# The tail of a fused attention and perception kernel: another order of its jobs, a fifth PSUM bank, results in tiles of their own

## The chip, the cores and the metric

The kernel runs on one core of one Trainium2 chip. The time is the device time of that core in microseconds, as a median of a few runs. The profile shows one more execution of the same kernel; its span runs from the first to the last instruction.

The engines are named as in the profile: PE (TensorE, matrix products), PEld (its weight loads), DVE (VectorE), ACT (ScalarE, which evaluates functions), POOL (GpSimd) and SP (SyncE, which issues the transfers here). PSUM has eight banks of 128 partitions by 512 float32 values; every product lands in one of them, and another engine has to read it out before the bank is used again.

## The reference

The input x has shape (4, 64, 64, 256): four images, 4096 pixels each, 256 channels. Everything is float32.

```python
# layer 0: attention of every pixel to every pixel of its image
q, k, v = x @ Wq + bq, x @ Wk + bk, x @ Wv + bv
attn = softmax(q @ k^T)
x = gamma * (attn @ v) + x
# layer 1: depthwise 3x3 convolution, two pointwise layers, local attention
perceived = conv3x3(x, w_perc, groups=256) + b_perc        # 768 channels
hid = gelu(w_up1 @ perceived + b_up1)                      # 512 channels
h = x + w_up2 @ hid + b_up2                                # 256 channels
q, k, v = split(w_qkv @ h + b_qkv)
w = softmax over the 3x3 neighbours of (q . k_neighbour) / 16
out = h + sum over the neighbours of w * v_neighbour
```

Neighbours outside the image have key and value zero, but they count in the softmax. So the result of a row needs the rows above and below it, both in the convolution and in the local attention.

## The kernel before

Channels lie on partitions. An image is cut into 8 blocks of 8 rows, 512 pixels each; over the four images this gives 32 blocks, which the code calls slots, 0 to 31. The function `unshifted` does everything, without subtracting a maximum in the softmax. It keeps a running sum `watched` of all intermediate values; at the end a flag `bad` says whether they stayed within bounds, and only if not a second, safe version runs. It does not run with these inputs, but the end of the program has to wait for the flag.

The **main loop** (lines 582 to 638) goes over the 32 slots. In each it runs the global attention of the slot's block on PE, and in between it weaves in layer 1 of blocks that are further back: the convolution of the block two slots back (`perceive`), the pointwise layers of the block three back (`hidden_jobs`), and the local attention of the block five back (`attention_jobs`). So at the end of the main loop these are left: the convolutions of blocks 30 and 31, the pointwise layers of 29, 30 and 31, and the local attention of 27 to 31. This is the **tail**, lines 641 to 656.

Instructions go to the engines in the order in which the Python code issues them (`tc.manual_schedule`); semaphores for tiles are put in by the framework. So the order of the jobs in the tail is the order of each engine's queue. The jobs are these; block numbers stand in brackets from here on.

- **hid** (`hidden`, four per block, line 310): six products of 512 columns into one bank on PE (two passes each, so twelve records), then a Gelu on ACT (line 319). They need all six results of the block's convolution.
- **upd** (`update`, two per block, line 321): four products of 512 columns into a bank, then one DVE instruction (line 331) that adds bias and x and writes one half of `h`.
- **new** (`local_values`, two per block, line 433): eight products of 256 columns that read both halves of `h`, and two DVE additions (line 446) to `lv` tiles.
- **guide** (two per block, line 395): two products of `h`, and an ACT instruction (line 405) that writes `lq`.
- **scores** (two, line 458): products of `h` and `lq`; an Exp on ACT (line 482); a multiplication with a mask on POOL (line 485). They read `h` of the next block too.
- **border and local_sum** (one job): four to eight small products, an Exp on ACT (line 429), and on POOL a multiplication (line 430), the sum of the two score tiles (line 494), small additions at the edge (lines 499 to 507) and an addition to `watched` (line 136).
- **local_denominator** (line 511, "ld" in the profile): one product with that sum, a reciprocal on DVE (line 515), and POOL's addition of it to `watched`.
- **local_product** (two, line 518, "lo"): twelve small products into a bank; DVE multiplies by the reciprocal (line 529) into a tile `o` of the two-buffer tag `lo`; POOL adds `o` to `watched` (`watch`, line 134); then `h` is added to `o` in place, on POOL for most blocks and on DVE for blocks 30 and 31 (line 532); and SP issues the transfer to the output (line 533).

`perceive` is a generator: for each of six results ACT does the first of nine taps (line 303), and DVE the other eight (line 307), one per call of `next`; so a block has 48 DVE steps. Since ACT's instruction is issued with the first step of its group, it stands in ACT's queue behind what was issued before.

In the tail each period k (29, 30, 31) runs the attention of block k-2 and the pointwise layers of block k alternately, with four steps of the convolution of block k+1 after each job. After the three periods come the attentions of blocks 30 and 31, and then the test of `watched` (lines 658 to 667). `job_bank` hands out the banks in turn; in the tail it takes "m" and "acc" (two banks each) alternately. The other four banks have the tag "e", for the energies of the global attention, which is over by then.

Of the kernel before, what the change touches and what calls it, by code (L numbers as in the profile page):

```python
# [8 lines left out]
F32 = mybir.dt.float32  # L9
AF = mybir.ActivationFunctionType  # L10
ALU = mybir.AluOpType
AX = mybir.AxisListType
PSUM = bass.MemoryType.PSUM

P = 128
# [5 lines left out]
NB = 512  # L21
# [4 lines left out]
TAPS = 9  # L26
MULT = 3
NPC = MULT * CH
# [3 lines left out]
GRP = P // CQK  # L32
NG = NT // GRP
NSLOT = B * NBLK

WATCH_MAX = 1.0e25

LAG_PERC, LAG_HID, LAG_ATT = 2, 3, 5
# [3 lines left out]
def attention_then_perception_kernel(  # L42
# [19 lines left out]
    nc = tc.nc  # L62
# [8 lines left out]
    ones = const.tile([P, P], F32, tag="ones", name="ones")  # L71
    watched = const.tile([P, NB], F32, tag="watched", name="watched")
    bad = const.tile([P, 1], mybir.dt.int32, tag="bad", name="bad")
# [3 lines left out]
    def unshifted():  # L77
        fctx = ExitStack()
        pool = fctx.enter_context(tc.tile_pool(name="fast", bufs=1))
        psum = fctx.enter_context(tc.tile_pool(name="fastp", bufs=1, space=PSUM))  # L80

        def tile_of(shape, tag, name, bufs=1):
            return pool.tile(shape, F32, tag=tag, name=name, bufs=bufs)

        def bank(tag, name):
            return psum.tile([P, NB], F32, tag=tag, name=name, bufs=2)
# [3 lines left out]
        turns = ["m"]  # L90

        def job_bank(name):
            turns.append(turns.pop(0))
            return bank(turns[-1], name)


# [21 lines left out]
        for half in range(2):  # L118
            m = near[half * W : (half + 1) * W]
            nc.gpsimd.affine_select(  # L120
                out=m, in_=m, compare_op=ALU.is_ge, fill=0.0,
# [3 lines left out]
                out=m, in_=m, compare_op=ALU.is_ge, fill=0.0,  # L125
# [8 lines left out]
        def watch(values):  # L134

            nc.gpsimd.tensor_tensor(watched, watched, values, ALU.add)  # L136
# [138 lines left out]
        percs, hids, hs = {}, {}, {}  # L275
        NPERC = NPC + 3

        def spare(name):
            return tile_of([P, TPB, C], "v", name, NBLK + 1).rearrange(
                "p (a t) c -> p a (t c)", a=2  # L280
            )

        def perceive(s):

            g = s % NBLK
            percs[s] = []
            for i in range(NPC):
                half, j = divmod(i, MULT)
                if s < NSLOT - LAG_PERC:
                    perc = tile_of([P, NB], "perc", f"perc_{s}_{i}", NPERC)  # L290
                else:

                    if i % 2 == 0:
                        pair = spare(f"perc_{s}_{i}")
                    perc = pair[:, i % 2, :]
                percs[s].append(perc)
                acc = perc.rearrange("p (h w) -> p h w", w=W)
                for tap in range(TAPS):
                    dy, dx = divmod(tap, 3)
                    win = xv[:, half, g * RB + dy : g * RB + dy + RB, dx : dx + W]  # L300
                    wt = wperc[:, half, j, tap : tap + 1]
                    if tap == 0:
                        nc.scalar.activation(  # L303
                            acc, win, AF.Identity, bias=bperc[:, half, j : j + 1], scale=wt
                        )
                    else:
                        nc.vector.scalar_tensor_tensor(acc, win, wt, acc, ALU.mult, ALU.add)  # L307
                        yield
# [86 lines left out]
        def guide(s, i):  # L395

            ps = job_bank(f"g_{s}_{i}")
            for kin in range(CH):
                nc.tensor.matmul(  # L399
                    ps, lhsT=wg[:, kin, bass.ts(i, P)], rhs=hs[s][:, kin, :],  # L400
                    start=(kin == 0), stop=(kin == CH - 1),
                )
            if i == 0:
                guides[s] = tile_of([P, CH, NB], "lq", f"lq_{s}")
            nc.scalar.activation(guides[s][:, i, :], ps, AF.Identity, bias=bg[:, i : i + 1])
# [42 lines left out]
        def pieces(s, odd):  # L448

            g = s % NBLK
            for t in range(-1 if odd else 0, TPB + 1, 2):
                lo, hi = max(0, (2 * t - 1) * W), min(NB, (2 * t + 3) * W)
                inside = 0 <= TPB * g + t < NT
                yield TPB * s + t if inside else None, slice(lo, hi)
# [54 lines left out]
        def local_denominator(s):  # L511
            ps = job_bank(f"ld_{s}")
            nc.tensor.matmul(ps, lhsT=ones, rhs=lsums.pop(s), start=True, stop=True)  # L513
            lrdens[s] = tile_of([P, NB], "rden", f"lrden_{s}", 2)
            nc.vector.reciprocal(lrdens[s], ps)  # L515
            watch(lrdens[s])

        def local_product(s, c):
            b, g = divmod(s, NBLK)
            ps = job_bank(f"lo_{s}_{c}")  # L520
            todo = [(t, cols, odd) for odd in (0, 1) for t, cols in pieces(s, odd)]
            todo = [x for x in todo if x[0] is not None]
            for i, (t, cols, odd) in enumerate(todo):
                nc.tensor.matmul(  # L524
                    ps[:, cols], lhsT=lvs[t][:, bass.ts(c, P)], rhs=near_ws[s, odd][:, cols],
                    start=(i == 0), stop=(i == len(todo) - 1), skip_group_check=True,
                )
            o = tile_of([P, NB], "lo", f"lo_{s}_{c}", 2)
            nc.vector.tensor_tensor(o, ps, lrdens[s], ALU.mult)  # L529
            watch(o)  # L530
            last = nc.vector if s >= NSLOT - 2 else nc.gpsimd
            last.tensor_tensor(o, o, hs[s][:, c, :], ALU.add)
            nc.sync.dma_start(out=out[b, :, c, bass.ts(g, NB)], in_=o)

        def hidden_jobs(k):

# [8 lines left out]
        def attention_jobs(a):  # L545
            if not 0 <= a < NSLOT:
                return [None] * 8
            return (
                [lambda i=i: guide(a, i) for i in range(CH)]
                + [lambda i=i: scores(a, i) for i in range(2)]  # L550
                + [lambda: (border(a), local_sum(a)), lambda: local_denominator(a)]
                + [lambda i=i: local_product(a, i) for i in range(CH)]
            )
# [28 lines left out]
        for slot in range(NSLOT):  # L582
            b, g = divmod(slot, NBLK)
            nc.sync.dma_start(
                out=xp[:, :, (1 + g * RB) * WP : (1 + (g + 1) * RB) * WP],
                in_=x[b, :, :, (1 + g * RB) * WP : (1 + (g + 1) * RB) * WP],
            )
            hid, upd, new = hidden_jobs(slot - LAG_HID)
            att = attention_jobs(slot - LAG_ATT)
            jobs = [  # L590
                hid[0], att[0], hid[1], att[1], hid[2], att[2], hid[3], att[3],
                upd[0], att[4], upd[1], att[5], att[6], att[7], *new,
            ]
            if slot == 1:
                combine = combine_steps()
                jobs = [lambda: next(combine)] * 4 + [None] * 12
# [5 lines left out]
            conv = perceive(slot - LAG_PERC) if slot >= LAG_PERC else iter(())  # L602
# [35 lines left out]
            finish(slot)  # L638


        turns.append("acc")
        for k in range(NSLOT - LAG_HID, NSLOT):
            hid, upd, new = hidden_jobs(k)
            att = attention_jobs(k - LAG_ATT + LAG_HID)
            ahead = k + LAG_HID - LAG_PERC
            conv = perceive(ahead) if ahead < NSLOT else iter(())
            for job in (
                att[0], hid[0], att[1], hid[1], att[2], hid[2], att[3], att[4], hid[3],
                att[5], *upd, att[6], att[7], *new,
            ):  # L650
                job()
                for _ in range(4):
                    next(conv, None)
        att, last = (attention_jobs(a) for a in (NSLOT - 2, NSLOT - 1))
        for job in (*att[:5], *last[:5], att[5], last[5], *att[6:], *last[6:]):
            job()

        good = tile_of([P, 2], "good", "good")
        for i, (holds, bound) in enumerate(((ALU.is_le, WATCH_MAX), (ALU.is_ge, -WATCH_MAX))):
            test = tile_of([P, NB], "o", f"test_{i}", 2)  # L660
            nc.vector.tensor_scalar(test, watched, bound, None, holds)
            nc.vector.tensor_reduce(good[:, i : i + 1], test, axis=AX.X, op=ALU.min)
        ps = bank("m", "good_sum")
        nc.tensor.matmul(ps[:, :2], lhsT=ones, rhs=good, start=True, stop=True)
        n_good = tile_of([P, 1], "n_good", "n_good")
        nc.vector.tensor_reduce(n_good, ps[:, :2], axis=AX.X, op=ALU.add)
        nc.vector.tensor_scalar(bad, n_good, 2.0 * P - 0.5, None, ALU.is_lt)
        fctx.close()
        return wv, bv, gam, wperc, bperc, wup1, bup1, wup2, bup2, blqk, blv

# [341 lines left out]
    with tc.manual_schedule():  # L1012
        wv, bv, gam, wperc, bperc, wup1, bup1, wup2, bup2, blqk, blv = unshifted()
# [50 lines left out]
```

## Time and profile before

| | |
|---|---|
| median of 3 runs | 3750.71 us (3748.83 to 3751.22) |
| the profiled run, its span | 3750.12 us, 3748.2 us |
| main loop's last product on PE (line 256) issued up to | 3545.98 us |
| period 29 on PE (up to the first guide of the next) | 3545.98 to 3603.71 us |
| period 30 | 3603.71 to 3658.43 us |
| period 31 | 3658.43 to 3701.89 us |
| attention of blocks 30 and 31, test, up to `bad` | 3701.89 to 3742.74 us |
| from `bad` to the end | 5.46 us |

The timeline lists the instructions of an engine with their start, their length, and, in brackets, how long the engine had been idle before and for what it waited. A line with x12 stands for twelve instructions in a row. The table by stages gives each engine's busy time in a stretch; PEclk there is the share of TensorE's full clock that was granted.

### The profile page before, as it was taken

How to read it: one execution, taken by the hardware profiler on the slowest of the kernel's cores; microseconds unless marked ns; L12 is line 12 of the kernel's file. 1: busy time of each engine (PE TensorE's matmuls, PEld its weight loads, DVE VectorE, ACT ScalarE, POOL GpSimd, SP SyncE). 2: the span in 40 equal slices, each digit the busy share in tenths (PEclk: the TensorE clock that was granted, in tenths of full speed). 3: DMA queues.
4: the chain of work that ended last, by engine and by line, in shares of the span. 5: the costliest groups of instructions: out<-in, count | busy, mean ns of one | idle time of the engine just before them, and what ended most of it. 6: DMA issues, size and time to landing. Idle time of an engine off the chain costs nothing.

```text
span 3748.2 us, 29155 instructions
## 1 busy us (share of the span) xinstructions
PE 3690.7 (98%) x11398; PEld 1767.7 (47%) x11398; DVE 2479.6 (66%) x2608; ACT 1164.2 (31%) x1271; POOL 724.2 (19%) x523
## 2 busy tenths in 40 slices
PE   8999999999999999999999999999999999999988
PEld 4334444554444444455444444445544444444455
DVE  2376666657677776756676677775677666677782
ACT  1223333223333333332333333333233333333221
POOL 0000012111122222112221222220122112222223
PEclk9999999999999999999999999999999999999999
DMA  4000000110000000021000000011100000000000
GB/s 106 15 17 9 3 0 15 37 40 9 15 15 15 15 15 15 1 44 41 15 3 12 15 15 15 15 23 35 28 15 15 15 1 15 15 15 12 6 6 24
DMA packets 101586, 68.99 MB, mean 18 GB/s; under 512 B 74432, under 2 KB 79552, under 8 KB 101312
## 3 DMA queue, kind: packets, MB, share of 16 engines
q1 hardware_dynamic: 98304, 63.47, 6.3%
q10 hardware_dynamic: 3136, 3.58, 0.3%
q8 instruction: 91, 1.49, 0.2%
q14 instruction: 55, 0.45, 0.0%
HBM read 46.04 MB, written 18.87 MB: 17 GB/s over the span
## 4 chain that ended last, share of the span: by engine, by line
PE 96%; DVE 2%; DMA 1%; ACT 0%; POOL 0%; issue 0%; SPq 0%; ACTq 0%; POOLq 0%; DVEq 0%
PE acc L233 47%; PE hid L315 18%; PE e L214 7%; PE dx L327 6%; PE lv L438 3%; PE s L465 3%; PE lo L524 3%; PE g L399 3%; PE v L177 3%; PE qk L156 1%; DVE perc L307 1%; PE dps L256 1%; PE ld L513 1%; DVE lrden L515 0%; DMA xc<-in_x 0%; PE c L422 0%
## 5 line engine op out<-in xcount | busy, mean ns | idle before, releaser
L233 PE MATMUL acc<-p,v 128*128 128x512 f32 x4096 | 1847.2, 595 | 3.2 <-DVE o L262 3.2
L307 DVE SCALAR_TENSOR_TENSOR perc<-xp,wperc,perc 128x512 f32<-128x512 f32 x1536 | 1371.8, 897 | 636.4 <-ACT perc L303 601.6
L233 PEld LDWEIGHTS acc<-p,v 128*128 128x128 f32 x4096 | 771.6, 190 | 904.7 <-issue 888.1
L222 ACT ACTIVATE p<-e 128x1024 f32<-128x1024 f32 x512 | 524.5, 1025 | 1670.3 <-PE e L214 821.4
L315 PE MATMUL hid<-perc,wup 128*128 128x512 f32 x1536 | 692.7, 600 | 2.7 <-DVE o L262 2.7
L247 DVE TENSOR_TENSOR den<-den,p 128x1024 f32<-128x1024 f32 x480 | 583.3, 1215 | 77.8 <-ACT p L222 74.5
L315 PEld LDWEIGHTS hid<-perc,wup 128*128 128x128 f32 x1536 | 281.7, 190 | 400.2 <-issue 389.5
L485 POOL TENSOR_TENSOR lp<-lp,near 128x512 f32<-128x512 f32 (+1 forms) x64 | 104.6, 1634 | 1393.5 <-ACT lp L482 1393.5
L214 PE MATMUL e<-qa,ka 32*128 32x512 f32 x2048 | 295.4, 643 | 4.4 <-DMA qa<-packed 2.4
L327 PE MATMUL dx<-hid,wup 128*128 128x512 f32 x512 | 235.7, 604 | 0.0
L222 ACT ACT_TABLE_LOAD x116 | 148.8, 1283 | 235.5 <-issue 120.8
L319 ACT ACTIVATE hid<-hid,bup 128x512 f32<-128x512 f32 x128 | 88.0, 687 | 385.9 <-PE hid L315 385.9
L258 DVE RECIPROCAL rden<-dps 128x512 f32<-128x512 f32 x32 | 107.4, 3358 | 121.5 <-PE dps L256 121.5
L214 PEld LDWEIGHTS e<-qa,ka 32*128 32x128 f32 x2048 | 81.4, 183 | 190.6 <-issue 182.1
L136 POOL TENSOR_TENSOR watched<-watched,lo 128x512 f32<-128x512 f32 x64 | 128.8, 2012 | 190.3 <-DVE lo L529 184.2
L319 ACT ACT_TABLE_LOAD x123 | 157.8, 1283 | 2.2
L327 PEld LDWEIGHTS dx<-hid,wup 128*128 128x128 f32 x512 | 92.5, 189 | 138.7 <-issue 115.2
L303 ACT ACTIVATE perc<-xp,bperc,wperc 128x512 f32<-128x512 f32 x192 | 154.2, 804 | 0.0
L331 DVE SCALAR_TENSOR_TENSOR h<-dx,bup,xp 128x512 f32<-128x512 f32 x64 | 48.0, 750 | 156.0 <-PE dx L327 155.8
L524 PE MATMUL lo<-lp,lv 128*128 128x64 f32 (+2 forms) x736 | 139.1, 341 | 5.0 <-DVE lrden L515 5.0
L524 PEld LDWEIGHTS lo<-lp,lv 128*128 128x128 f32 x736 | 120.0, 196 | 48.6 <-issue 31.8
L515 DVE RECIPROCAL lrden<-ld 128x512 f32<-128x512 f32 x32 | 107.4, 3357 | 51.4 <-PE ld L513 51.4
(82 smaller groups left out, 2023.4 us busy)
## 6 DMA issues: line engine op xcount, KB each, us to landing
xp<-in_x SPq DMA_DIRECT2D x32, 528.0 KB, 4.8
xc<-in_x SPq DMA_DIRECT2D x64, 256.0 KB, 3.8
out<-lo SPq DMA_DIRECT2D x64, 256.0 KB, 2.0
qa<-packed SPq DMA_DIRECT2D x128, 64.0 KB, 3.5
ka<-st SPq DMA_DIRECT2D x128, 16.0 KB, 1.8
packed<-st SPq DMA_DIRECT2D x32, 64.0 KB, 1.9
wup<-in_w_up ACTq DMA_DIRECT2D x1, 1536.0 KB, 8.2
wup<-in_w_up ACTq DMA_DIRECT2D x1, 512.0 KB, 8.6
```

Source lines behind the costliest of these rows:

```text
L136: nc.gpsimd.tensor_tensor(watched, watched, values, ALU.add)
L177: nc.tensor.matmul(ps[:, i * C : (i + 1) * C], lhsT=xc[:, kin, bass.ts(2 * pair + i, P)], rhs=wv[:, kin, :], start=(kin == 0), stop=(kin = ...
L214: nc.tensor.matmul(e[:, j, :], lhsT=key[rows, :], rhs=queries[s][rows, :], start=True, stop=True,)
L222: nc.scalar.activation(p, energies[s, G][:, 2 * half : 2 * half + 2, :], AF.Exp)
L233: nc.tensor.matmul(accs[s][c], lhsT=v[:, 2 * half + i, bass.ts(c, P)], rhs=p[:, i, :], start=(first and i == 0), stop=(G == NG - 1 and hal ...
L247: nc.vector.tensor_tensor(den, den, p, ALU.add)
L303: nc.scalar.activation(acc, win, AF.Identity, bias=bperc[:, half, j : j + 1], scale=wt)
L307: nc.vector.scalar_tensor_tensor(acc, win, wt, acc, ALU.mult, ALU.add)
L315: nc.tensor.matmul(ps, lhsT=wup1[:, i, bass.ts(d, P)], rhs=percs[s][i], start=(i == 0), stop=(i == NPC - 1),)
L319: nc.scalar.activation(hids[s][:, d, :], ps, AF.Gelu, bias=bup1[:, d : d + 1])
L327: nc.tensor.matmul(ps, lhsT=wup2[:, d, bass.ts(c, P)], rhs=hids[s][:, d, :], start=(d == 0), stop=(d == NHC - 1),)
L524: nc.tensor.matmul(ps[:, cols], lhsT=lvs[t][:, bass.ts(c, P)], rhs=near_ws[s, odd][:, cols], start=(i == 0), stop=(i == len(todo) - 1), sk ...
```

## The change

The change touches the tail alone.

1. **Order.** Period k runs the pointwise layers of block k first, with all convolution steps of block k+1 between these jobs, and only then the two `new` jobs and, from period 29 on, the attention of block k-1. Period 29 has to do two attentions, of blocks 27 (still interleaved, in a slightly different order) and 28; period 30 does that of block 29; period 31 does none. In period 29 there are twelve jobs with four steps each, in period 30 six jobs with eight steps each. The last section, with blocks 30 and 31, keeps its order.
2. **Banks.** `job_bank` goes round "m", "e", "acc", "m", "acc", where "e" is the first of the four banks of the energies.
3. **Results.** For blocks 30 and 31 the addition of `h` writes to a tile of the two-buffer tag "o" and no longer to the tile that `watch` reads.
4. **Test.** Two comparisons and two reductions become two comparisons, of which the second multiplies in the first, and one reduction; the reduction after the product with `ones` goes.

```diff
         def job_bank(name):
             turns.append(turns.pop(0))
+            if turns[-1] == "e":
+                return psum.tile([P, GRP, NB], F32, tag="e", name=name, bufs=1)[:, 0, :]
             return bank(turns[-1], name)
...
             watch(o)
-            last = nc.vector if s >= NSLOT - 2 else nc.gpsimd
-            last.tensor_tensor(o, o, hs[s][:, c, :], ALU.add)
-            nc.sync.dma_start(out=out[b, :, c, bass.ts(g, NB)], in_=o)
+            engine, res = nc.gpsimd, o
+            if s >= NSLOT - 2:
+                engine, res = nc.vector, tile_of([P, NB], "o", f"res_{s}_{c}", 2)
+            engine.tensor_tensor(res, o, hs[s][:, c, :], ALU.add)
+            nc.sync.dma_start(out=out[b, :, c, bass.ts(g, NB)], in_=res)
...
-        turns.append("acc")
+        turns[:] = ["m", "e", "acc", "m", "acc"]
+        def step(conv, n):
+            for _ in range(n):
+                next(conv, None)
+
+        convs = {k: perceive(k) for k in range(NSLOT - LAG_PERC, NSLOT)}
+        att = [attention_jobs(a) for a in range(NSLOT)]
         for k in range(NSLOT - LAG_HID, NSLOT):
             hid, upd, new = hidden_jobs(k)
-            att = attention_jobs(k - LAG_ATT + LAG_HID)
-            ahead = k + LAG_HID - LAG_PERC
-            conv = perceive(ahead) if ahead < NSLOT else iter(())
-            for job in (
-                att[0], hid[0], att[1], hid[1], att[2], hid[2], att[3], att[4], hid[3],
-                att[5], *upd, att[6], att[7], *new,
-            ):
+            conv = convs.get(k + 1, iter(()))
+            first = k == NSLOT - LAG_HID
+            a, b = att[k - 2], att[k - 1]
+            if first:
+                jobs = [a[0], hid[0], a[1], hid[1], *a[2:4], hid[2], *a[4:5], hid[3], a[5], *upd]
+                rest = [*a[5+1:], *new, *b]
+            elif k < NSLOT - 1:
+                jobs = [*hid, *upd]
+                rest = [*new, *b]
+            else:
+                jobs, rest = [*hid, *upd], [*new]
+            n = -(-NPC * (TAPS - 1) // len(jobs))
+            for job in jobs:
                 job()
-                for _ in range(4):
-                    next(conv, None)
-        att, last = (attention_jobs(a) for a in (NSLOT - 2, NSLOT - 1))
+                step(conv, n)
+            for job in rest:
+                job()
+        att, last = att[NSLOT - 2 :]
         for job in (*att[:5], *last[:5], att[5], last[5], *att[6:], *last[6:]):
             job()
 
-        good = tile_of([P, 2], "good", "good")
-        for i, (holds, bound) in enumerate(((ALU.is_le, WATCH_MAX), (ALU.is_ge, -WATCH_MAX))):
-            test = tile_of([P, NB], "o", f"test_{i}", 2)
-            nc.vector.tensor_scalar(test, watched, bound, None, holds)
-            nc.vector.tensor_reduce(good[:, i : i + 1], test, axis=AX.X, op=ALU.min)
+        test = [tile_of([P, NB], "o", f"test_{i}", 2) for i in range(2)]
+        nc.vector.tensor_scalar(test[0], watched, -WATCH_MAX, None, ALU.is_ge)
+        nc.vector.scalar_tensor_tensor(
+            test[1], watched, WATCH_MAX, test[0], ALU.is_le, ALU.mult
+        )
+        good = tile_of([P, 1], "good", "good")
+        nc.vector.tensor_reduce(good, test[1], axis=AX.X, op=ALU.min)
         ps = bank("m", "good_sum")
-        nc.tensor.matmul(ps[:, :2], lhsT=ones, rhs=good, start=True, stop=True)
-        n_good = tile_of([P, 1], "n_good", "n_good")
-        nc.vector.tensor_reduce(n_good, ps[:, :2], axis=AX.X, op=ALU.add)
-        nc.vector.tensor_scalar(bad, n_good, 2.0 * P - 0.5, None, ALU.is_lt)
+        nc.tensor.matmul(ps[:, :1], lhsT=ones, rhs=good, start=True, stop=True)
+        nc.vector.tensor_scalar(bad, ps[:, :1], P - 0.5, None, ALU.is_lt)
```

## The prediction, made before the changed kernel was run

> **What bounds the kernel now.** I read the page first, then the table by stages over the tail, then the timelines of PE, DVE, ACT and POOL in it, and last the chain of waits at the end. The page says that PE carries the kernel, except in the last slices:
>
> ```profile
> PE 3690.7 (98%) x11398; PEld 1767.7 (47%) x11398; DVE 2479.6 (66%) x2608; ACT 1164.2 (31%) x1271; POOL 724.2 (19%) x523
> PE   8999999999999999999999999999999999999988
> ```
>
> The main loop keeps its code, so I take its 3546 us as given. The table by stages cuts the tail at the first guide of each period, at `bad`, and at the end. Its columns are stretch, length, then the busy time (and instructions) of PE, PEld, DVE, ACT and POOL, PEclk, and the transfers:
>
> ```profile
> 3546.00:3603.70 57.70, 48.99 (x143) 27.69 (x142) 54.16 (x60) 16.09 (x20) 15.56 (x12) 0.91 0.00 1
> 3603.70:3658.43 54.73, 48.67 (x144) 27.87 (x142) 47.05 (x57) 14.81 (x19) 13.76 (x12) 0.91 0.03 10
> 3658.43:3701.89 43.46, 43.46 (x144) 24.65 (x143) 7.75 (x9) 10.60 (x13) 13.92 (x14) 1.00 0.05 18
> 3701.89:3742.74 40.85, 27.61 (x123) 19.47 (x121) 14.94 (x18) 6.73 (x11) 19.95 (x22) 0.88 0.09 33
> ```
>
> Period 31, with the same PE work and no convolution, is all PE: 43.46 us. Periods 29 and 30 are 14.2 and 11.3 us longer: there DVE, with 48 convolution steps, ends last. This is how it holds PE up (PE timeline, then DVE timeline, period 29; in brackets the idle time before):
>
> ```profile
> 3589.60 3.90 PE L524 MATMUL lo<-lp,lv 128*128 128x192 f32 x12 [2.49 <-DVE lrden L515]
> 3594.08 0.70 PE L438 MATMUL lv<-wlv,h 128*128 128x256 f32 x2 [0.58 <-DVE h L331]
> 3597.76 6.12 PE L438 MATMUL lv<-wlv,h 128*128 128x256 f32 x14 [2.98 <-DVE h L331]
> ```
> ```profile
> 3567.41 18.87 DVE L307 SCALAR_TENSOR_TENSOR perc<-xp,wperc,perc 128x512 f32<-128x512 f32 x20 [0.66 <-ACT perc L303]
> 3586.19 3.35 DVE L515 RECIPROCAL lrden<-ld 128x512 f32<-128x512 f32 x1
> 3589.46 3.90 DVE L307 SCALAR_TENSOR_TENSOR perc<-xp,wperc,perc 128x512 f32<-128x512 f32 x4
> 3593.28 0.75 DVE L331 SCALAR_TENSOR_TENSOR h<-dx,bup,xp 128x512 f32<-128x512 f32 x1
> ```
>
> PE needs `h`, and the instruction that writes `h` stands in DVE's queue behind 44 of the 48 steps. The waits cost twice: the twelve products at 3589.60 take 3.90 us where the other half (3584.98) took 2.12, and the fourteen at 3597.76 take 6.12 us where sixteen take 3.62 in period 31. In the last section the end hangs on DVE and POOL taking turns (chain of waits: start, length, what):
>
> ```profile
> 3731.26 0.69 DVE lo L529
> ...
> 3732.09 1.28 POOL watched L136
> ...
> 3733.39 0.24 DVE lo L532
> ```
>
> **What the Trainium skill says.** (1) "TensorE: Matmul & The Clock Gate", section "Part 1: The HAM clock gate": the array's clock falls to half after an idle window of about 3.4 us and comes back after a busy one. The trace agrees: PEclk is 0.50 in each microsecond from 3590 to 3593 and from 3597 to 3603, behind these waits. (2) Same page and section: the queues of ScalarE, VectorE and GpSimdE are strict FIFO. The trace agrees: in the tail each of these engines shows its instructions in the order of the code. (3) "GPSIMD Engine Reference", section "1. Specifications": GpSimd shares its SBUF interfaces with VectorE and they contend when a VectorE instruction has two SBUF inputs. The trace agrees: a convolution step takes 0.76 us, and 1.65 beside POOL's 1.75 at 3577.02.
>
> **The change part by part.** All durations are of the profiled execution, span 3748.2; its own run took 3750.12, and the runs shown 3748.83 to 3751.22, so I add the difference to the median 3750.71.
>
> *Bank "e" in period 29: nothing.* hid(29)'s first job waited 2.66 us for an "acc" bank (DVE, line 262) and would start at 3547.7. But what ends the period is DVE's queue, which starts its convolution at 3553.31 in either case, after the writes to x (line 266).
>
> *Convolution steps ahead, period 29: -0.66 us.* There were twelve jobs with four steps each before the last four jobs, and there are now; DVE's queue (36 steps, reciprocal, 4, `h`, 4, `h`, 4) is unchanged. Both scores come before the third hid, so ACT issues the first tap of group three at 3563.6 and not 3566.57, and the wait of 0.66 us goes. `h` is complete at 3597.05 (was 3597.71), the `new` products end at 3603.05 (was 3603.71). They stay slow: PE has run dry by 3586.3.
>
> *Attention of 28 moved ahead of hid(30): hid(30) starts at 3621.6 and not 3605.43.* With nothing beside it, it runs as block 30's does in the last section, whose first guide starts at 3701.89. Counted from there: guides and scores with a wait of 0.45 us and border end at +8.44 (3710.33); then ACT's Exp, POOL's masks, `pad`, sum (line 494, +10.39) and edge (line 499, to +11.94). So `ld` starts at +12.1 and PE stands 3.7 us. Then `ld` 0.86 and two lo 3.92, and half a clock over one 3.4 us window, 1.7 us, as an estimate from the 0.50 stretches: +18.6. Of the moved instructions, DVE's reciprocal (3.35) and two multiplications (1.3), POOL's eleven (about 12 us) and SP's two issues (0.36 each, landing in 2.0) have their engines to themselves: nothing else is in SP's queue in the tail, and DVE idles from about 3604.
>
> *Convolution of 31: `h`(30) complete at 3661.1 and not 3652.52.* Its first tap now stands in ACT's queue behind the Gelu of hid(30)'s first job, and DVE's steps wait for it. From a hid's start (3605.43) to its Gelu 5.41, then 0.6 and 0.8 (lines 319 and 303, as spaced at 3605.69 and 3606.28): DVE starts 6.8 us after hid, at 3628.4. In the changed order 40 steps and two `h` precede the end of `h`; eight steps take 6.26 undisturbed (3607.11), since POOL is quiet: 5 x 6.26 + 1.4 = 32.7. The later groups never wait: first taps follow at 5.15 us, DVE takes 6.26. Here the change gains: before, 3607.11 to 3652.52 was 45.4. But PE ends upd(30) at 3621.6 + 20.6 + 6.9 = 3649.1 and stands until `h` arrives, but for one 0.7 us product.
>
> *From `h`(30) to the last section: 56.1 us and not 49.4.* `new` slowed again 6.0; attention of 29 18.6 as above; hid 4 x 5.15 = 20.6; upd 6.87; then `new` waits 0.6 for `h`(31), no lo lying between; `new` 3.45. Sum 56.1, so the last section's first guide starts at 3717.2 and not at 3701.89: **+15.3 us**.
>
> *The last section: -3.9 us.* Up to the end of its last reciprocal (3727.86) nothing changes. Then four multiplications and four additions follow on DVE: first pair 3727.8 to 3729.1, second to 3730.5. The third multiplication needs `watch` of the first (POOL: 3729.35 to 3730.6): to 3731.5. The third addition reuses the first tag "o" tile, whose transfer, issued at 3729.2 and landing in 2.0, is out at 3731.3. The fourth multiplication needs PE's last lo, which ends at 3732.87: 3733.0; its addition ends at 3734.4. Its transfer lands at 3736.5, and that is a **new wait**: the second test tile is that tile. Behind it in DVE's queue are only the test and `bad`, for which the program's end waits. Comparison 0.75, as an estimate the row of line 331; reduction 0.69; PE and rest 0.9: `bad` ends at about 3738.8, not 3742.74. Bounds: 0 if transfers land late, -5.5 if the wait costs nothing.
>
> Sum: 15.3 - 3.9 = +11.4; span 3759.6, **time 3762.1 us**, 0.30% more.
>
> **The rivals.**
> (a) *The round trips come cheaper.* The clock might stay up in both `ld` waits (2 x 1.7) and recover earlier behind both `new` (2 x 1.5), and the end gain 1 us more: +4.0, 3754.7. For it: the wait of 2.66 us at 3547.8 left PEclk at 1.00. Against: 3.0 us before line 513 at 3722.66 brought it to 0.50.
> (b) *The end gains nothing*, because the test waits for the last transfers and POOL and DVE slow each other: +15.3, 3766.0. For: POOL's additions stretched to 2.24 us beside DVE (3480.82). Against: POOL's last addition, not slowed, would end at 3735.1, and transfers to `out` landed in 2.0 to 3.2 us.
> (c) *Faster: the queues do not hold block 30 behind block 28.* Place: PE's hid(30) runs in the gaps of attention 28 and 29, and DVE starts the convolution of 31 near 3607. Price: with `h`(30) at about 3651.8 and PE done with upd(30) at 3649.1, the +15.3 shrinks to +6.0; covering both waits of 3.66 and their 1.7 takes off 10.7; with -3.9 that is -8.6: 3742.1. It decides from the point that hid(30) starts before `ld`(28). Against it: the order of the queues seen before.
>
> **How the numbers follow.** Chances: forecast 0.62, (a) 0.13, (b) 0.18, (c) 0.07. A difference of 0.2%, 7.5 us, is about what a measurement of this kernel tells from no change. Range: the forecast with the clock's bounds (3.4 either way on the `ld` waits, 3 on `new`) and the end's; from 3754, which takes in (a), to 3768, which takes in (b); (c) and little else is outside. Slower by over 0.2% are (b) and nearly all of the forecast, 0.78; within it (a) and the forecast's edge, 0.15; faster (c), 0.07.
>
> **What would show it.** In the trace after: DVE's first step of block 31 near 3628; between the last upd(30) product and `new` some 12 us of PE waiting; two waits of about 3.7 us before line 513 in periods 29 and 30; the last section's first guide near 3717; from there to `bad` 37 us, not 40.9. I am wrong if hid(30) starts before 3615, if the convolution of 31 starts without waiting for a Gelu, or if the last section starts before 3710.

## The result

| | median | lowest to highest | runs |
|---|---|---|---|
| before | 3749.21 us | 3748.36 to 3751.22 | 6 |
| after | 3762.22 us | 3760.17 to 3763.55 | 6 |

The ratio after to before is 1.0034, with a 95% interval of 1.0021 to 1.0046: the change makes the kernel 13.0 us slower. The forecast was 3762.1 us, and +11.4 us against the median then known (3750.71); with three more runs the kernel before stands 1.5 us lower. So the time was met more closely than the increase, which was 1.6 us larger than forecast.

The page after shows no more instructions on any engine, and less busy time of PE in the last two slices:

```profile
PE 3691.7 (98%) x11398; PEld 1768.4 (47%) x11398; DVE 2477.3 (66%) x2606; ACT 1159.0 (31%) x1267; POOL 722.9 (19%) x523
...
PE   8999999999999999999999999999999999999977
```

The table by stages, cut as before at the first guide of periods 29 and of the next ones, at `bad`, and at the end (columns as in the table of before):

```profile
3543.80:3601.25 57.45, 47.58 (x143) 26.71 (x142) 54.43 (x60) 16.10 (x20) 15.73 (x12) 0.88 0.00 1
3601.25:3666.48 65.23, 49.09 (x143) 27.89 (x142) 42.04 (x55) 12.25 (x17) 14.44 (x14) 0.87 0.04 16
3666.48:3717.17 50.69, 45.74 (x143) 25.75 (x142) 8.75 (x12) 8.03 (x11) 11.69 (x11) 0.97 0.03 11
3717.17:3754.85 37.68, 27.49 (x123) 19.34 (x121) 16.22 (x16) 6.73 (x11) 20.42 (x21) 0.91 0.08 28
```

The first stretch is as long as before (57.7 us then), the second 10.5 us longer, the third 7.2 us longer, the fourth 3.2 us shorter. The stretches hold the same PE instructions (the counts differ by one at most), so their difference is waiting and slow clock: in the second PE is idle for 16.1 us instead of 6.1, in the third for 5.0 instead of 0, and there it is also busy 2.3 us longer. Where PE waits is in its timeline (start, length, what; in brackets how long it had been idle and for what):

```profile
3591.51 1.22 PE L440 MATMUL lv<-wlv,h 128*128 128x256 f32 x2 [7.41 <-DVE h L333]
3595.19 6.22 PE L440 MATMUL lv<-wlv,h 128*128 128x256 f32 x14 [2.46 <-DVE h L333]
...
3613.78 1.13 PE L515 MATMUL ld<-lsum,ones 128*128 128x512 f32 x2 [4.09 <-POOL lsum L501]
3614.75 5.76 PE L526 MATMUL lo<-lp,lv 128*128 128x192 f32 x24
3620.34 20.76 PE L317 MATMUL hid<-perc,wup 128*128 128x512 f32 x48
...
3653.96 1.22 PE L440 MATMUL lv<-wlv,h 128*128 128x256 f32 x2 [5.99 <-DVE h L333]
3660.79 5.86 PE L440 MATMUL lv<-wlv,h 128*128 128x256 f32 x14 [5.61 <-DVE h L333]
...
3679.02 1.46 PE L515 MATMUL ld<-lsum,ones 128*128 128x512 f32 x2 [4.09 <-POOL lsum L501]
```

(Line numbers after are 2 to 4 higher: 440 is `new`, 515 `ld`, 526 lo, 317 hid, 333 the write of `h`.) Two waits for POOL of 4.09 us have come in, and the wait for `h`(30) has grown from 0.6 + 3.0 to 6.0 + 5.6 us. On DVE, the convolution of block 31 begins after an idle time that ACT ends:

```profile
3628.45 24.79 DVE L309 SCALAR_TENSOR_TENSOR perc<-xp,wperc,perc 128x512 f32<-128x512 f32 x32 [7.16 <-ACT perc L305]
3653.16 0.74 DVE L333 SCALAR_TENSOR_TENSOR h<-dx,bup,xp 128x512 f32<-128x512 f32 x1
3653.82 6.25 DVE L309 SCALAR_TENSOR_TENSOR perc<-xp,wperc,perc 128x512 f32<-128x512 f32 x8
3659.99 0.74 DVE L333 SCALAR_TENSOR_TENSOR h<-dx,bup,xp 128x512 f32<-128x512 f32 x1
```

Executions differ by some microseconds in how long the main loop takes: its last product (line 256, 258 after) starts at 3545.12 in the profile before and at 3542.94 after, and between 3541.6 and 3546.7 in the runs below. So I count from that product, in microseconds:

| | before | forecast | after |
|---|---|---|---|
| `h`(29) complete | 52.6 | 51.9 | 52.2 |
| hid(30) starts | 60.3 | 76.5 | 77.4 |
| convolution of 31 starts on DVE | 62.0 | 83.3 | 85.5 |
| `h`(30) complete | 107.4 | 116.0 | 117.8 |
| first guide of the last section | 156.8 | 172.1 | 174.2 |
| `bad` complete | 197.6 | 209.0 | 211.9 |
| end | 203.1 | 214.5 | 217.6 |

The tail is 14.5 us longer, and the main loop of this one execution 2.2 us shorter, which makes the 12.3 us between the two spans (3748.2 and 3760.5 us).

### The profile page after: what moved, and what is told of

Its sections match the earlier page's. It is cut to its first block, busy times and chain, and to the rows that moved or that the text cites. A ratio compares the mean times of both kernels' runs of the same rounds, so it can differ in the third digit from the quotient of the medians.

```text
span 3760.5 us, 29152 instructions
## 1 busy us (share of the span) xinstructions
PE 3691.7 (98%) x11398; PEld 1768.4 (47%) x11398; DVE 2477.3 (66%) x2606; ACT 1159.0 (31%) x1267; POOL 722.9 (19%) x523
## 4 chain that ended last, share of the span: by engine, by line
PE 96%; DVE 2%; DMA 0%; POOL 0%; ACT 0%; issue 0%; SPq 0%; ACTq 0%; DVEq 0%
PE acc L235 47%; PE hid L317 17%; PE e L216 7%; PE dx L329 6%; PE lo L526 3%; PE lv L440 3%; PE s L467 3%; PE v L179 3%; PE g L401 3%; DVE perc L309 2%; PE qk L158 2%; PE ld L515 1%; PE dps L258 1%; PE c L424 0%; DVE rden L260 0%
## 5 line engine op out<-in xcount | busy, mean ns | idle before, releaser
L329 PEld LDWEIGHTS dx<-hid,wup 128*128 128x128 f32 x512 | 92.5, 189 | 138.7 <-issue 116.0
L440 PE MATMUL lv<-wlv,h 128*128 128x256 f32 x512 | 130.9, 401 | 21.9 <-DVE h L333 21.9
L138 POOL TENSOR_TENSOR watched<-watched,den 128x512 f32<-128x512 f32 x32 | 40.5, 1267 | 513.2 <-DVE den L251 513.2
```

Of the source, the lines that this page charges most:

```text
L329: nc.tensor.matmul(ps, lhsT=wup2[:, d, bass.ts(c, P)], rhs=hids[s][:, d, :], start=(d == 0), stop=(d == NHC - 1),)
L440: nc.tensor.matmul(ps[:, i * C : (i + 1) * C], lhsT=hs[s][:, kin, bass.ts(t, P)], rhs=wlv[:, kin, :], start=(kin == 0), stop=(kin == CH - 1),)
```

## The experiments

The theory is that of the prediction: the order holds the convolution of 31 behind the attention of 28 and a Gelu of hid(30), so that `h`(30) comes late, and it leaves PE alone with two round trips over ACT and POOL. Times against the kernel before are against its runs on the same chip in the same batch.

**The parts one by one.** `e1_order` is the kernel before with part 1 of the diff, `e2_end` with parts 3 and 4, `e3_banks` with part 2. For e1 the round keeps its four banks:

```diff
-        turns[:] = ["m", "e", "acc", "m", "acc"]
+        turns.append("acc")
```

> The kernel before with the new order of the tail alone: four banks in turn, results and test as before. Theory (the order holds the convolution of block 31 behind the attention of 28 and a Gelu of hid(30), and bares two POOL round trips): the whole delay of the last section stays and nothing is given back at the end, so 17 us more than the kernel before, about 3766.5, with the last section's first guide some 17.5 us later, counted from the end of the main loop. Rival (the delay comes from the five banks or from the result and test tiles): within 2 us of the kernel before.

Measured: 3766.21 us, before 3748.06, ratio 1.0045 (1.0031 to 1.0059), +18.2 us. The last section's first guide is at 174.4 us from the main loop's last product, 17.7 us later than before.

> The kernel before with the results of blocks 30 and 31 in tiles of their own and the shorter test alone. Theory: the last section is 3.2 us shorter, as between the two profiles, 3746.0. Rival (the new wait for the output transfers eats the gain, and what the changed kernel shows comes from elsewhere): no change, 3749.2.

Measured: 3744.82 us, before 3748.06, ratio 0.9993 (0.9984 to 1.0001), -3.2 us. The interval just reaches 1, but the trace shows the gain where it was expected: from the last section's first guide to `bad` 37.4 us instead of 40.9. All of it comes from part 3: from the end of the last reciprocal to the first comparison it is 8.1 us instead of 11.6. The shorter test of part 4 gives nothing here: from the first comparison to `bad` it takes 3.30 us, before 3.28, since its second comparison waits 0.56 us for an output transfer. In `e7_both` and `e9_h_at_28` below, whose results lie in tiles apart from those of the test, that wait is gone and it takes 2.8 us.

> The kernel before with the fifth bank in the round alone. Theory (the periods end with h on DVE, so waits for banks are covered): within 1 us of the kernel before, although the 2.7 us wait before the first hid and the two waits of 2.5 us before a lo go. Rival (those waits and the slow clock behind them are paid in full): 2.7 + 2 x (2.5 + 1.9) = 11.5 us less, 3738.

Measured: 3747.67 us, before 3748.06, ratio 0.9998 (0.9990 to 1.0006). The waits for banks are gone from PE, and what took their place is in its timeline:

```profile
3579.78 4.08 PE L526 MATMUL lo<-lp,lv 128*128 128x192 f32 x24
3591.41 1.22 PE L440 MATMUL lv<-wlv,h 128*128 128x256 f32 x2 [7.54 <-DVE h L333]
```

Before, PE waited 2.49 us between the two halves of lo; now it does both at once and waits 7.54 us for `h`, which is there only 0.4 us sooner. In this one trace the tail is 2.1 us shorter, mostly because `new` was back at full clock sooner (14 products in 4.82 and 5.36 us, before 6.12 and 6.01). That differs between executions: behind the same wait they take 6.22 us in the profile after and 4.90 in that of `e8_gelu_ahead`.

So the order costs 18.2, the end gives 3.2, the banks 0.4: together +14.5, the same as the tail of the profile after shows, and within the two batches' uncertainty of the +13.0 measured. The order alone makes the kernel slower.

**The held convolution.** In e4 the first 20 steps of the convolution of 31 stand between the first jobs of the attention of 28:

```diff
-            for job in rest:
+            for i, job in enumerate(rest):
                 job()
+                if first and 4 <= i < 9:
+                    step(convs[NSLOT - 1], 4)
```

> The changed kernel with twenty of the 48 convolution steps of block 31 put between the first five jobs of the attention of block 28, four behind each. Theory: DVE starts the convolution near 3605 and not 3628, h(30) is complete some 8 us sooner, while hid(30) starts as before; so 8.5 us less than the changed kernel, about 3753.7. Rival (the loss is the bare POOL waits and the slow clock, not the held convolution): within 2 us of the changed kernel.

Measured: 3756.77 us, before 3748.06, ratio 1.0022 (1.0013 to 1.0031): +8.7 us, where the changed kernel had +13.0, so 4.3 us came back, and 6.0 us in the trace (first guide of the last section at 168.3). The intervals of the two ratios overlap, so the trace has to decide here: that the held convolution costs is confirmed, the size was half of the 8.5 us expected. DVE starts 23.7 us sooner (61.8), but `h`(30) is there only 5.4 us sooner (112.4). DVE's timeline shows why:

```profile
3603.41 19.33 DVE L309 SCALAR_TENSOR_TENSOR perc<-xp,wperc,perc 128x512 f32<-128x512 f32 x20 [2.44 <-ACT perc L305]
3622.65 3.35 DVE L517 RECIPROCAL lrden<-ld 128x512 f32<-128x512 f32 x1
3626.20 1.29 DVE L531 TENSOR_TENSOR lo<-lo,lrden 128x512 f32<-128x512 f32 x2 [0.20 <-DVE lrden L517]
3627.41 25.32 DVE L309 SCALAR_TENSOR_TENSOR perc<-xp,wperc,perc 128x512 f32<-128x512 f32 x28
3652.64 1.40 DVE L333 SCALAR_TENSOR_TENSOR h<-dx,bup,xp 128x512 f32<-128x512 f32 x2
```

The 48 steps take 44.7 us here, and 37.3 in the changed kernel, where POOL is quiet during them; and all 48, the reciprocal and the two multiplications now stand in front of `h`. For POOL it is the same: `ld`(28) waits 5.78 us for it instead of 4.09.

**The second round trip.** In e5 the attention of 29 goes back into period 31:

```diff
             elif k < NSLOT - 1:
-                jobs = [*hid, *upd]
-                rest = [*new, *b]
-            else:
                 jobs, rest = [*hid, *upd], [*new]
+            else:
+                jobs = [a[0], hid[0], a[1], hid[1], *a[2:4], hid[2], a[4], hid[3], a[5], *upd]
+                rest = [*a[6:], *new]
```

> The changed kernel with the attention of block 29 put back into period 31, alternating with the pointwise layers of 31; that of block 28 stays ahead. Theory: the second bare wait for POOL (4.1 us), the slow clock behind it (2.1), the 0.45 for lq and the 0.4 before new(31) go: 6.9 us less than the changed kernel, about 3755. Rival (only the held convolution costs, and PE would wait anyway): no change against the changed kernel, 3762.

Measured: 3754.46 us, before 3747.66, ratio 1.0017 (1.0011 to 1.0024): +6.8 us, so 6.2 us less than the changed kernel's +13.0 (here too the intervals overlap, by a little). In the trace it is 7.8 us between `h`(30) and the last section (48.7 us, in the changed kernel 56.4). From the end of new(30) to the last section PE has no wait left, and `ld` and lo run at full clock:

```profile
3697.07 1.02 PE L515 MATMUL ld<-lsum,ones 128*128 128x512 f32 x2
...
3704.79 4.08 PE L526 MATMUL lo<-lp,lv 128*128 128x192 f32 x24
```

The second round trip costs about what the sum said (6.9).

**The table of functions.** From hid(30) to the first step on DVE I had counted 6.8 us; it took 8.1. ACT's timeline after shows a load of its function table (1.28 us) that starts only when PE has ended the first hid:

```profile
3625.74 1.28 ACT L321 ACT_TABLE_LOAD   x1 [15.46 <-PE hid L317]
3627.03 0.69 ACT L321 ACTIVATE hid<-hid,bup 128x512 f32<-128x512 f32 x1
3627.62 0.80 ACT L305 ACTIVATE perc<-xp,bperc,wperc 128x512 f32<-128x512 f32 x1
```

Before, the Gelu loads of the tail ran ahead of the wait (at 3622.20 the load came straight behind the first tap, 2.6 us before the Gelu). e8 puts a Gelu of one column ahead:

```diff
             n = -(-NPC * (TAPS - 1) // len(jobs))
+            if not first:
+                early = tile_of([P, 1], "early", f"early_{k}", 2)
+                nc.scalar.activation(early, bup1[:, 0:1], AF.Gelu, bias=bup1[:, 0:1])
```

> The changed kernel with a Gelu of one column, on data that has long been there, ahead of hid(30) and of hid(31), so that the table is loaded before PE ends the first hid. Theory (the term of 6.8 us from hid(30) to DVE's first step measured 8.1 because the load stood behind the wait for PE): 6.8 us again, and h(30) 1.3 us sooner, counted from hid(30). Rival (the 1.3 us come from the Gelu or the first tap itself): 8.1 us as before.

Measured, from one profiled execution: hid(30) starts at 3619.13, DVE's first step at 3625.96, 6.83 us; `h`(30) is complete 39.1 us behind the start of hid(30), in the changed kernel 40.4. Its time, 3760.02 us, is a single one and says nothing on 1.3 us.

```profile
3609.24 1.28 ACT L669 ACT_TABLE_LOAD   x1
3610.53 0.29 ACT L669 ACTIVATE early<-bup 128x1 f32<-128x1 f32 x1
3624.54 0.69 ACT L321 ACTIVATE hid<-hid,bup 128x512 f32<-128x512 f32 x1 [13.71 <-PE hid L317]
```

The Trainium skill, "ScalarE: Activation LUTs", section "What ACT_TABLE_LOAD costs", gives about 1.28 us for the load; the trace agrees. What makes a load stand before or behind a wait was not tried.

**Orders that use the finding.** If `h`'s place in DVE's queue and bare round trips set the tail, an order that mends both should be faster than either kernel. e6 does this with `h` after 30 steps (period 29) and 35 (period 30):

```diff
+            if k == NSLOT - LAG_HID:
+                jobs = [a[0], hid[0], a[1], hid[1], a[2], hid[2], a[3], a[4], hid[3], a[5]]
+                n, m = 3, 2
...
+                jobs = [a[5], hid[0], a[6], hid[1], a[7], hid[2], hid[3]]
+                n, m = 5, 3
             for job in jobs:
                 job()
                 step(conv, n)
+            for job in upd:
+                job()
+            rest = [*a[6:], *new] if k == NSLOT - LAG_HID else [*new]
+            if k < NSLOT - 1:
+                rest += b[:5]
+            for job in rest:
+                job()
+                step(conv, m)
```

> The changed kernel with another order: both upd jobs of a block come after 30 (period 29) or 35 (period 30) of the 48 convolution steps, so that DVE writes h when PE is done with it; the rest of the steps lies beside new and the first five attention jobs of the next block, and the two lo and ld stand between the hid of the following period. Theory (what sets the tail is h behind convolution steps in DVE's queue and bare POOL waits): the last section starts 147 to 152 us after the end of the main loop (the kernel before: 157), and with the shorter end the kernel takes about 3738 (3735 to 3742), less than both. Rival (the tail is held by PE's own work and its clock, order matters little): at or above the kernel before less 3.2 us, 3745 or more.

Measured: 3746.54 us, before 3747.66, ratio 0.9995 (0.9986 to 1.0003). By the expectation this is a miss: the time lies where the rival put it, and the last section starts at 158.0, not at 147 to 152. But the trace does not show PE held by its own work:

```profile
3583.76 3.95 PE L440 MATMUL lv<-wlv,h 128*128 128x256 f32 x16 [0.45 <-DVE h L333]
...
3601.38 2.07 PE L515 MATMUL ld<-lsum,ones 128*128 128x512 f32 x2 [5.39 <-POOL lsum L501]
...
3643.07 6.18 PE L440 MATMUL lv<-wlv,h 128*128 128x256 f32 x16 [6.34 <-DVE h L333]
...
3662.07 2.08 PE L515 MATMUL ld<-lsum,ones 128*128 128x512 f32 x2 [4.55 <-POOL lsum L501]
```

The wait for `h`(29) is cured (0.45 us, full clock: 3.95). But I had put `ld` in front of the next hid, so both round trips stand bare again, and I had counted the steps of period 30 at 0.78 us: beside POOL's work 35 of them took 31.3 us, 0.89 each. `h`(30) came 6 us after PE needed it, and some 4 of these are the slower steps (35 times 0.11).

e7 takes the guides, scores and border of block 30 forward, so that the second round trip has PE work beside it and the last section has only block 31's left:

```diff
+        run([*new, *c[:5]], conv, 2)
+        run([*d[:2], *c[5:]])
+        hid, upd, new = hidden_jobs(NSLOT - 1)
+        run([hid[0], d[3], *hid[1:], *upd, d[2], d[4], *new])
+        run([*e[:5], d[5], e[5], *d[6:], *e[6:]])
```

(`c`, `d`, `e` are the attentions of 29, 30, 31; `run` issues the jobs with so many steps after each. The results go to the free tag "perc".)

> As e6, and the guides of block 30 come before hid(31), its odd scores after the first hid(31), and the even ones and the border before new(31), so that the last section has only block 31's guides, scores and border ahead of ld; results of blocks 30 and 31 go to four tiles apart from those of the test. Theory: PE's wait for the convolution of 31 is filled, the last section loses some 8 us of its chain and the wait for the output transfers 0.6: 21 us less than the kernel before, about 3728 (3724 to 3734). Rival (the last section is bound by DVE and POOL after the last reciprocal, so moving block 30's work ahead gives nothing): as e6.

Measured: 3738.97 us, before 3747.66, ratio 0.9974 (0.9964 to 0.9985), -8.7 us. Less than the 21 expected, since it carries e6's first bare round trip (PE waits 5.39 us) and its late `h`(30); 7.6 us less than e6, so the rival falls. PE still waits 6.15 us for `h`(30):

```profile
3643.49 6.37 PE L440 MATMUL lv<-wlv,h 128*128 128x256 f32 x16 [6.15 <-DVE h L333]
```

e9 changes this alone:

```diff
-        run([b[5], hid[0], b[6], hid[1], b[7], hid[2], hid[3]], conv, 5)
+        run([b[5], hid[0], b[6], hid[1], b[7], hid[2], hid[3]], conv, 4)
         run(upd)
-        run([*new, *c[:5]], conv, 2)
+        run([*new, *c[:5]], conv, 3)
```

> As e7, with one number changed: in period 30, 28 of the 48 convolution steps of block 31 come before the upd jobs and not 35; the 20 left lie beside new(30) and the attention of 29, three behind each job. In e7, PE waits 6.2 us for h(30) and then runs new(30) at half clock for 6.4 us instead of 3.5. Theory (h's place in DVE's queue is what holds PE): seven steps of some 0.88 us less in front of h, so the wait and its slow clock go almost wholly, and the convolution of 31 still ends before hid(31) begins: 8 to 9 us less than e7, about 3730. Rival (DVE's whole work up to the end of the convolution of 31 sets the start of hid(31), wherever h lies): within 2 us of e7, 3739.

Measured: 3732.88 us, before 3748.89, ratio 0.9958 (0.9944 to 0.9971), **-16.0 us**. That is 6.1 us less than e7, or 7.3 if each is taken against the kernel before in its own batch; 8 to 9 were expected. The rival falls, and `h`'s place does set PE's time:

```profile
3638.92 3.95 PE L440 MATMUL lv<-wlv,h 128*128 128x256 f32 x16 [1.20 <-DVE h L333]
...
3657.04 1.12 PE L515 MATMUL ld<-lsum,ones 128*128 128x512 f32 x2 [2.26 <-POOL lsum L501]
```

The wait fell from 6.15 to 1.20 and `new` from 6.37 to 3.95 us, together 7.4; 0.9 of it went into the wait for POOL (2.26, in e7 1.38), whose masks and sums now have more convolution steps beside them. This version beats both kernels.

## Why the prediction was right

- **Period 29 gains 0.66 us.** Near in size (0.4 us from the main loop's last product to `h`(29)), and DVE is fed without a gap, but this is luck: the cause was the other of the two terms. With the order alone (first line, e1) the gap stays and `h`(29) comes at 52.5 us; with the fifth bank alone (second line, e3) it goes and `h`(29) comes at 52.2:

```profile
3567.02 18.75 DVE L307 SCALAR_TENSOR_TENSOR perc<-xp,wperc,perc 128x512 f32<-128x512 f32 x20 [0.66 <-ACT perc L303]
```
```profile
3551.03 32.58 DVE L309 SCALAR_TENSOR_TENSOR perc<-xp,wperc,perc 128x512 f32<-128x512 f32 x36
```

  The step that failed is "Bank "e" in period 29: nothing". With it the first hid starts 2.8 us sooner, and so does what stands behind it in ACT's queue: the first tap of group three comes 18.53 us after the main loop's last product, in e1 and before 21.45. To the time of the whole kernel the bank waits are worth nothing that `e3_banks` can show.
- **Attention of 28 bare, +18.6 us to hid(30).** It took 19.1. `ld` came 12.5 us behind the first guide and not 12.1: I had taken the pattern from the last section, where the Exp's table load runs ahead of the scores; here it waited for them.
- **First step 6.8 us behind hid(30).** The term that was mis-sized: 8.1 us, by the 1.28 us of a table load behind a wait. e8 shows it.
- **40 steps and two `h`, 32.7 us.** 32.3. That POOL is quiet during them was right, and e4 shows its price: 44.7 us for 48 steps beside POOL's work, and 37.3 without.
- **56.1 us from `h`(30) to the last section.** 56.4, and its terms hold one by one, to half a microsecond; e5 takes 6.2 us of it away (7.8 in the trace) by hiding the second round trip.
- **The last section, -3.9 us.** -3.2 in the profile, and -3.2 in e2's time. The step that failed is the pace of DVE and POOL: I let DVE's pairs run and took `watch` at 1.27 us, but beside each other both slow down, four `watch` taking 6.62 us and DVE's additions 0.97 to 1.39 instead of 0.69. So DVE's last addition, counted from the section's first guide, ends 0.7 us later than forecast (0.3 of it because the last reciprocal ends that much later, behind an `ld` of 2.08 us, before 1.80), and the last transfer lands 0.7 us later. POOL's last `watch` is late too and releases the first comparison; the second waits 0.56 us more for the transfer, the new wait that was forecast:

```profile
3751.56 0.43 DVE L677 TENSOR_SCALAR test<-watched 128x512 f32<-128x512 f32 x1 [1.15 <-POOL watched L138]
3752.54 0.69 DVE L678 SCALAR_TENSOR_TENSOR test<-watched,test 128x512 f32<-128x512 f32 x1 [0.56 <-DMA out<-res]
```

- **The sum.** +15.3 - 3.9 was forecast, +17.5 - 3.2 came in the tail of the profile (and 0.2 behind `bad`). Both errors go the same way, 2.9 us; that the time itself was met to 0.1 us is luck: the median that the forecast was added to was 1.5 us too high, which made up for an increase 1.6 us too small.
- **The rivals.** (a) falls: the clock was at half behind each long wait (both lo behind `ld`(28) take 5.76 us, in period 31 of before, at full clock, 4.08; PEclk is 0.50 from 3615 to 3618). How long PE has to stand for that is not settled by these traces: before, half clock followed waits of 2.49 and 2.98 us, less than the window of 3.4 us named in the prediction, while the wait of 2.66 us near 3548 left it at 1.00. (b) falls as stated, the end gains 3.2 us, though its mechanism, POOL and DVE slowing each other, was there with some 0.5 us. (c) falls: the queues ran in the order of the code, and hid(30) started behind lo(28).

## What to carry to other kernels

When an engine runs its queue in order, what holds up the engine that bounds the kernel can be one short instruction's place in another engine's queue: moving two writes of 0.7 us seven convolution steps forward was worth 6 to 7 us here (e9 against e7). Before moving a chain over several engines to a place of its own, look for independent work of the bounding engine to stand beside it; without it, each round trip over ACT and POOL costs its length and then the half clock behind it, here 4.1 + 1.8 us (in the profile after, from `ld` to the next hid 6.56 us; at full clock `ld` and lo took 4.8).

## What was not expected of the hardware

An ACT table load can start ahead of its instruction's wait or behind it, in the same kernel and for the same line (after, line 484: behind a wait of 1.98 us for PE at 3607.55, with none at 3721.51): 1.28 us that are hidden or not (e8). Which of the two happens, and why, stays open. And a convolution step on DVE costs 0.78 us with POOL quiet and up to 1.0 us on average beside POOL's elementwise work (17 steps in 16.98 us in e9), which made some 4 of the 6 us that PE waited for `h`(30) in e6.
